# Holding back part of a weight load behind the first gather, and moving one tile's first steps forward, in a routed feed-forward kernel

## The chip, the cores and the metric

One core of a Trainium2 chip runs the whole kernel. Its engines are TensorE (PE in the profile; its weight loads are PEld), VectorE (DVE), ScalarE (ACT), GpSimd (POOL) and SyncE (SP), which here only issues transfers. The metric is the device time of one execution in microseconds, as the median of several runs. The kernel before takes 59.47 us (three runs, 58.83 to 59.89).

## The reference

```python
def _L0_cond_ref(inputs, initial_state):        # x and cond
    rates = relu(inputs) * 0.001
    c = initial_state[:, None, :] + cumsum(rates, axis=1)
    fl = floor(c)
    prev = concatenate([floor(initial_state)[:, None, :], fl[:, :-1, :]], axis=1)
    return (fl - prev) / 0.001                   # spikes

def _L0_ffn_ref(x, router_w, w1, w2):           # E = 8 experts, K = 2, HID 256, FFN 1024
    probs = softmax(x_flat @ router_w.T)
    top_v, top_i = top_k(probs, 2); top_v = top_v / sum(top_v)
    for k in range(2):
        # each token goes to expert top_i[:, k], if there is room for it
        h = gelu(expert_in @ w1[e], approximate=False)
        y = h @ w2[e]
        out = out + y[token] * (gate * keep)
    return out

return x + _L0_ffn_ref(_L0_cond_ref(x, cond), router_w, w1, w2)
```

x is 32 sequences of 64 steps and 256 channels, so 2048 tokens. A spike (0 or 1000) comes only where the running sum of a channel passes a whole number, which is rare: most tokens have no spike at all, a few have one, fewer have two. The product of such a token with w1 is one row of w1, or the sum of two rows, times 1000.

## The kernel before

**States and waves.** x lies in SBUF as 16 blocks of 128 tokens. A block's running sums are matrix products (`summed_up`, `begun`) and a floor (`floor`). Eight blocks make a *wave*; there are two. `chain(w, between)` takes one wave from its states to its indices: it finds the tokens that have a spike (`live`, `rk`), packs them (`sel`, `seld`, then the matmul of L431 and its copy to `spt`, L440), multiplies with the router's weights (L451), picks the two best experts (`best`, L473; `oh`), counts places (L485 to L494), compares them with row numbers (`strike`, L388), and multiplies that out to indices of rows of w1 (`collect`, L513; `idx`, L536 and L542).

**Tiles.** Each wave has two tiles `q`, of four experts with 32 rows each: tile 0 is wave 0 with experts 0 to 3, tile 1 wave 0 with 4 to 7, and tiles 2 and 3 the same of wave 1. For each tile GpSimd issues two gathers of rows of w1 (`bring`, L522): the first spike's rows, and the second's for those tokens that have one. `add_rows` (L891, VectorE) adds the two in place, `turn_rows` (L903, TensorE) turns the sum in pieces of 128 columns, `hidden` (L910, ScalarE) takes the GELU, and `second` (L920, TensorE) multiplies with w2 of the tile's four experts. A *quarter* is 256 of the 1024 columns, a *pair* two of the eight pieces.

**What stands between the steps.** `chain` calls `between` at named points, and what is called there is put into the engines' lists at that point. In the first wave these are the second wave's states (`second_states`); in the second wave it is `others`, with spins (`spin`, L307: products of zeros that nothing reads), VectorE's `lead` and `choices` (which of a token's two experts is first and which second), and, after the first index of the wave (`rows0`), `first_tile`: tile 0's sums, four spins, turns and GELU, and the first quarter of its second product. The indices of tile 3 (`rows1`) are multiplied out behind it. After both waves come tile 0's other three quarters, tile 1's sums, `choices(1)`, `members_told`, `weighed`, `counted` (L721), and then the other tiles.

**Who sets the order.** TensorE, VectorE, ScalarE and GpSimd run in the order of the code (`manual_schedule` names these four). SP is not named: the order of its transfers is set by a planner at build time, which keeps what depends on what and may otherwise change places. On SP stand, in this kernel, most of x, then w2 in twelve loads (experts 0 to 3 whole, 1 MB each; the first halves of experts 4 to 7, then their second halves, 0.5 MB each), then `out` = x in two stores. The last two steps add the tiles' results by indirect stores onto those rows of `out` that have spikes, and wait for these two.

```python
    parts = [(e, slice(0, FC)) for e in range(E // 2)]
    for s in (slice(0, FC // 2), slice(FC // 2, FC)):
        parts += [(e, s) for e in range(E // 2, E)]
```

The matmul's operand `w2_sb` is one tile, and each load writes its own part of it.

Of the kernel before, what the change touches and what calls it, by code (L numbers as in the profile page):

```python
# [13 lines left out]
AF = mybir.ActivationFunctionType  # L14
# [15 lines left out]
@with_exitstack  # L30
def adaln_ffn_kernel(
    ctx: ExitStack,
    tc: tile.TileContext,
    x: bass.AP,
    cond: bass.AP,
    router_w: bass.AP,
    w1: bass.AP,
    w2: bass.AP,
    out: bass.AP,
):  # L40

    nc = tc.nc
    P = 128  # L50
    B, T, H = x.shape
    E, _, FF = w1.shape
    N = B * T
    NB = N // P
    HC = H // P
    FC = FF // P
    WE = HC * FF
    assert WE == FC * H
    of = out.rearrange("b t h -> (b t) h")

    const = ctx.enter_context(tc.tile_pool(name="const", bufs=1))
    wpool = ctx.enter_context(tc.tile_pool(name="weights", bufs=1))
    dram = ctx.enter_context(tc.tile_pool(name="dram", bufs=1, space=bass.MemoryType.DRAM))


    cond_sb = const.tile([B, H], F32, name="cond_sb")
    nc.scalar.dma_start(cond_sb, cond)
    x_sb = const.tile([P, NB, H], F32, name="x_sb")
    xf = x.rearrange("b t h -> (b t) h").rearrange("(i p) h -> p i h", p=P)
    rw_sb = const.tile([E, H], F32, name="rw_sb")  # L70
    for queue, s in (
        (nc.sync, slice(0, 1)),
        (nc.scalar, slice(2, 4)),
        (nc.sync, slice(1, 2)),
        (nc.sync, slice(4, 6)),
        (nc.sync, slice(6, 8)),
        (nc.sync, slice(8, 12)),
        (nc.sync, slice(12, 16)),
    ):
        queue.dma_start(x_sb[:, s, :], xf[:, s, :])  # L80
        if s.start == 8:
            nc.sync.dma_start(rw_sb, router_w)
    w2_sb = wpool.tile([P, E * WE], F32, name="w2_sb")

    parts = [(e, slice(0, FC)) for e in range(E // 2)]
    for s in (slice(0, FC // 2), slice(FC // 2, FC)):
        parts += [(e, s) for e in range(E // 2, E)]
    for e, s in parts:
        nc.sync.dma_start(
            w2_sb[:, e * WE : (e + 1) * WE].rearrange("p (c h) -> p c h", c=FC)[:, s, :],  # L90
            w2[e].rearrange("(c p) h -> p c h", p=P)[:, s, :],
        )

    for s in (slice(0, 8), slice(8, 16)):
        nc.sync.dma_start(of.rearrange("(i p) h -> p i h", p=P)[:, s, :], x_sb[:, s, :])

    spk_dram = dram.tile([N, H], F32, name="spk_dram")
    y_dram = dram.tile([tiles_at_most(N, E, 2) * P, H], F32, name="y_dram")
    shape = (B, T, H, E, FF)
    bad_i = const.tile([P, 1], I32, name="bad_i")  # L100

    sparse(tc, x.rearrange("b t h -> (b t) h"), x_sb, cond_sb, rw_sb, w1.rearrange("e h f -> (e h) f"), w2_sb, out, bad_i, shape)
    bad = nc.values_load(
        bad_i[0:1, 0:1],
        min_val=0,
        max_val=16 * P,
        skip_runtime_bounds_check_because="it is a count of flags, at most 16 in a partition",
    )
    with tc.If(bad > 0):
        general(tc, x_sb, cond_sb, rw_sb, w1, w2_sb, out, spk_dram, y_dram, shape)  # L110


SB = 32
RE = 32


@with_exitstack
def sparse(ctx, tc, xf, x_sb, cond_sb, rw_sb, w1r, w2_sb, out, bad_i, shape):

# [8 lines left out]
    nc = tc.nc  # L130
    P = 128
# [5 lines left out]
    FC = FF // P  # L137
    WE = HC * FF
# [3 lines left out]
    W = 2  # L142
# [25 lines left out]
    warm = sc.tile([P, 4], F32, name="warm")  # L168
    nc.vector.memset(warm, 0.0)  # L169
    nc.scalar.activation(warm, warm, AF.Sqrt)  # L170
    zero = sc.tile([P, 1], F32, name="zero")
# [131 lines left out]
    def spin(n, cols=512):  # L303

        for _ in range(n):
            spun[0] += 1
            nc.tensor.matmul(wide[spun[0] % 2][:, :cols], busy.to_broadcast([P, P]), busy.to_broadcast([P, cols]), start=True, stop=True)  # L307
# [87 lines left out]
    def chain(w, between):  # L395
# [30 lines left out]
        for j in range(JW):  # L426
            t = w * JW + j
# [8 lines left out]
                        stop=True,  # L436
                    )
        for j in range(JW):
            copy = nc.vector.tensor_copy if j == 0 else nc.scalar.copy
            copy(spt[:, w * JW + j].rearrange("p c s -> p (c s)"), mid[j][:, : HC * P])  # L440
        between("spikes")

# [68 lines left out]
        def collect(out, q, s):  # L511
            for n, j in want:
                tell(  # L513
                    out,
                    slots_to_rows(n, q, j),
                    info[:, tiles(n)[j], s],
                    start=(n, j) == want[0],
                    stop=(n, j) == want[-1],
                )

        def bring(q, k):
            nc.gpsimd.indirect_dma_start(  # L522
                out=w1g[:, w, q, k, :],
                out_offset=None,
                in_=w1r,
                in_offset=bass.IndirectOffsetOnAxis(ap=idx[w][q][k], axis=0),
                bounds_check=E * H - 1,
                oob_is_err=False,
            )

        for q in range(Q):
            if q:
                for n in reversed(members[w]):
                    strike(n, q)
            collect(first[:, q : q + 1], q, slice(0, 1))
            nc.vector.tensor_scalar(  # L536
                idx[w][q][0], first[:, q : q + 1], w1_row[:, q, 0:1], E * H - 1.0, ALU.add, ALU.min
            )
            bring(q, 0)
            collect(rest[:, q], q, slice(1, 4))  # L540
            nc.vector.tensor_tensor(far[:, w, q : q + 1], rest[:, q, 0:1], w1_row[:, q, 1:2], ALU.add)
            nc.vector.scalar_tensor_tensor(  # L542
                idx[w][q][1], rest[:, q, 2:3], -FAR, far[:, w, q : q + 1], ALU.mult, ALU.add
            )
            bring(q, 1)
            between(f"rows{q}")
# [123 lines left out]
    def choices(w):  # L670
        js = slice(w * JW, (w + 1) * JW)
        nc.vector.tensor_scalar(valid[:, js], lg_w[w][:, :, E], 0.0, None, ALU.is_lt)
        nc.vector.tensor_tensor(ohk[:, 0, js], lg_w[w][:, :, :E], bc(best[:, js, 0], E), ALU.is_equal)
        nc.vector.tensor_tensor(ohk[:, 0, js], ohk[:, 0, js], ohj[w], ALU.mult)
        nc.vector.tensor_tensor(ohk[:, 1, js], ohj[w], ohk[:, 0, js], ALU.subtract)

    def others(at):
        if at == "ranks":
            spin(2)
        if at == "slots":  # L680

            nc.vector.tensor_reduce(most, cum[0].rearrange("p e j -> p j e"), AX.X, ALU.max)
            nc.vector.tensor_scalar(over, most, TOP + RE, None, ALU.is_gt)
            nc.vector.tensor_tensor(more, oh[:, 0], over.unsqueeze(1).to_broadcast([P, E, JW]), ALU.mult)
            lead(0)
            choices(0)
        if at == "spikes":
            spin(2)
        if at == "logits":
            told(1)  # L690
            spin(1)
        if at == "places":
            spin(1)
            lead(1)
            nc.scalar.activation(warm, zero[:, 0:1].to_broadcast([P, 4]), AF.Gelu)
            spin(1)
        if at == "rows0":
            first_tile()
            nc.scalar.activation(g1, gap, AF.Exp)
            nc.scalar.activation(warm, zero[:, 0:1].to_broadcast([P, 4]), AF.Gelu)  # L700
# [187 lines left out]
    def add_rows(u, s):  # L888
        w, q = order[u]
        g = w1g[:, w, q]  # L890
        nc.vector.tensor_tensor(g[:, 0, s], g[:, 0, s], g[:, 1, s], ALU.add)  # L891
# [7 lines left out]
    def turn_rows(u, cs):  # L899

        w, q = order[u]
        for c in cs:
            nc.tensor.transpose(turning(u, c, c + 1), w1g[:, w, q, 0, c * P : (c + 1) * P], ident)  # L903

    def hidden(u, cs):

        if u not in hts:
            hts[u] = big.tile([P, FC, P], F32, name=f"ht{u}")
        lo, hi = cs[0], cs[-1] + 1
        nc.scalar.activation(  # L910
            hts[u][:, lo:hi, :].rearrange("p c s -> p (c s)"), turning(u, lo, hi), AF.Gelu, scale=INV_DT
        )
# [52 lines left out]
    def quarter(n):  # L965
        return slice(n * FF // 4, (n + 1) * FF // 4)
# [4 lines left out]
    def pair(n):  # L971
        return range(2 * n, 2 * n + 2)
# [6 lines left out]

    def first_tile():  # L980

        for n in range(4):
            add_rows(0, quarter(n))
        spin(4)
        for n in range(3):
            turn_rows(0, pair(n))
            hidden(0, pair(n))
        second(0, pair(0))
        turn_rows(0, pair(3))
        hidden(0, pair(3))  # L990
# [10 lines left out]
    second(0, pair(1))  # L1001
    for n in range(2):
        add_rows(1, half(n))
    choices(1)
    members_told()
    weighed()
    second(0, pair(2))
# [442 lines left out]
```

## Time and profile before

| | |
|---|---|
| median of the runs | 59.47 us |
| the profiled execution: own time, span | 61.9 us, 59.8 us |
| busy: PE, PEld, DVE, ACT, POOL | 47.1, 28.1, 36.7, 26.8, 26.6 us |
| granted TensorE clock, mean | 0.90 |
| transfers | 15.45 MB; SP's queue 12.33, GpSimd's 2.65 |
| issue to landing, gathers of w1 | 6.7 to 7.6 us |
| issue to landing, loads of w2 | 9.0 to 12.7 us |

The profile is of one execution, whose own time is 61.9 us; the span runs from its first to its last instruction, and 2.1 us lie around it. Times in it count from the span's start. A row of a group or of the timeline names line, engine and operation, then output and inputs; what stands in brackets is how long the engine had been idle and which instruction ended that. A busy TensorE is modelled and not TensorE at its peak. The clock row gives the granted share of full speed in tenths.

### The profile page before, as it was taken

Reading aid. Unit: us, or ns where it says so; the run is one execution under the profiler, and the core shown is the slowest. Engines: PE = TensorE matmul, PEld = TensorE weight load, DVE = VectorE, ACT = ScalarE, POOL = GpSimd, SP = SyncE. Lnnn points to the kernel's source line nnn. Section 1 sums busy time; section 2 is a strip of 40 time slices with the busy share of each in tenths; the row PEclk is TensorE's granted clock in tenths of the full one; section 3 lists DMA queues with packets and bytes.
Section 4 is the critical chain, followed back from the end, with each engine's and each line's share of the span. In section 5 each row is a group of like instructions: output and inputs, shape, how many; then the busy total and the mean of one; then the engine's idle time right before and its main releaser. Section 6 shows DMA issues by size and latency. Waiting matters only on the chain.

```text
span 59.8 us, 1524 instructions
## 1 busy us (share of the span) xinstructions
PE 47.1 (79%) x513; PEld 28.1 (47%) x515; DVE 36.7 (61%) x205; ACT 26.8 (45%) x59; POOL 26.6 (44%) x69
## 2 busy tenths in 40 slices
PE   3999996999596684789997998999999999740000
PEld 1347773778353353247435574675585445210000
DVE  4787099546477771779006999999989874040000
ACT  0868486177952203751609939395009910000000
POOL 5899989495057778237406700000066000606000
PEclk9999999999999999555569999999999999997555
DMA  0699999999999999999999999999922300010200
GB/s 0 158 372 344 357 346 355 351 350 346 346 357 345 347 362 379 364 363 347 348 347 392 348 357 376 377 381 384 364 84 88 93 11 0 11 68 16 75 16 0
DMA packets 14047, 15.45 MB, mean 258 GB/s; under 512 B 1057, under 2 KB 13385, under 8 KB 14032
## 3 DMA queue, kind: packets, MB, share of 16 engines
q1 hardware_dynamic: 12368, 12.33, 63.5%
q0 software_dynamic: 1344, 2.65, 12.4%
q10 hardware_dynamic: 320, 0.30, 1.4%
q8 instruction: 6, 0.10, 0.7%
q14 instruction: 9, 0.07, 0.4%
HBM read 14.98 MB, written 2.36 MB: 290 GB/s over the span
## 4 chain that ended last, share of the span: by engine, by line
PE 69%; DVE 14%; issue 4%; ACT 2%; POOL 1%; POOLq 1%; DVEq 0%
PE wide L920 23%; PE wide L333 11%; PE wide L307 8%; PE wide L903 5%; PE mid L431 4%; PE mid L952 4%; DVE hit L388 3%; DVE ge L351 2%; DVE w1g L891 2%; PE wide L336 2%; ACT ht L910 2%; PE mid L513 2%; PE mid L333 1%; PE mid L903 1%; POOL out_dram L956 1%
## 5 line engine op out<-in xcount | busy, mean ns | idle before, releaser
L920 PE MATMUL wide<-w_sb,ht 128*32 128x256 f32 x256 | 16.3, 398 | 0.3 <-ACT ht L910 0.3
L522 POOL DMA_INDIRECT w1g<-in_L_ffn_w_dram,idx x8 | 8.8, 1098 | 9.2 <-DVE idx L542 5.1
L920 PEld LDWEIGHTS wide<-w_sb,ht 128*32 128x32 f32 x256 | 7.7, 113 | 6.2 <-issue 1.3
L333 PE MATMUL wide<-rel,trib 128*128 128x256 f32 x28 | 10.0, 472 | 0.0
L307 PE MATMUL wide<-busy 128*128 128x512 bf16 x15 | 6.6, 561 | 1.2 <-DVE warm L169 0.9
L910 ACT ACTIVATE ht<-wide 128x512 f32<-128x512 f32 (+1 forms) x8 | 4.0, 542 | 7.6 <-PE wide L903 7.6
L333 PEld LDWEIGHTS wide<-rel,trib 128*128 128x128 f32 x28 | 5.5, 228 | 2.1 <-POOL slot L229 0.9
L831 POOL DMA_INDIRECT xg<-in_x_dram,idx_x x2 | 2.0, 1012 | 9.7 <-DVE idx_s L830 9.3
L328 ACT ACTIVATE rel<-x_sb 128x512 f32<-128x512 f32 (+1 forms) x9 | 5.2, 580 | 1.8 <-DMA x_sb<-in_x_dram 1.6
L351 DVE TENSOR_SCALAR_CACHE_REDUCE ge<-wide 128x256 bf16<-128x256 f32 x11 | 4.3, 421 | 2.2 <-PE wide L336 2.0
L891 DVE TENSOR_TENSOR w1g<-w1g 128x512 f32<-128x512 f32 (+1 forms) x10 | 5.3, 579 | 0.0
L956 POOL DMA_INDIRECT out_dram<-o,idx_s x2 | 2.0, 1018 | 7.0 <-DVE o L955 7.0
L937 ACT ACTIVATE junk<-x_sb,xlim 128x1024 bf16<-128x1024 f32 x4 | 4.6, 1148 | 0.0
L903 PE MATMUL wide<-ident,w1g 128*128 128x128 f32 x28 | 4.3, 297 | 0.0
L903 PEld LDWEIGHTS wide<-ident,w1g 128*128 128x128 f32 x28 | 3.5, 153 | 1.0 <-DVE g L270 0.4
L281 POOL MEMSET w1g<- 128x1024 f32 x4 | 3.7, 949 | 0.0
L952 PE MATMUL mid<-y,back 128*128 128x256 f32 x8 | 2.8, 428 | 0.8 <-DVE y L930 0.8
L336 PE MATMUL wide<-con,selt 96*128 96x256 bf16 x14 | 3.3, 273 | 0.0
L536 DVE TENSOR_SCALAR idx<-mid,w_row 128x1 uint32<-128x1 f32 x4 | 0.9, 218 | 3.9 <-PE mid L513 3.6
L388 DVE TENSOR_TENSOR hit<-small,iota_r 128x256 bf16<-128x256 f32 x6 | 2.4, 419 | 1.1 <-PE small L494 1.1
L307 PEld LDWEIGHTS <-busy 128*128 128x128 bf16 x17 | 1.6, 120 | 2.9 <-issue 2.0
L930 DVE COPY y<-wide 128x256 f32<-128x256 f32 x4 | 1.7, 418 | 1.7 <-PE wide L920 1.7
(215 smaller groups left out, 82.2 us busy)
## 6 DMA issues: line engine op xcount, KB each, us to landing
w_sb<-in_L_ffn_w_dram SPq DMA_DIRECT2D x4, 1024.0 KB, 9.0
w_sb<-in_L_ffn_w_dram SPq DMA_DIRECT2D x8, 512.0 KB, 12.4
out_dram<-x_sb SPq DMA_DIRECT2D x2, 1024.0 KB
x_sb<-in_x_dram SPq DMA_DIRECT2D x2, 512.0 KB, 6.4
x_sb<-in_x_dram SPq DMA_DIRECT2D x2, 256.0 KB
x_sb<-in_x_dram SPq DMA_DIRECT2D x2, 128.0 KB, 2.4
x_sb<-in_x_dram ACTq DMA_DIRECT2D x1, 256.0 KB
w1g<-in_L_ffn_w_dram,idx POOLq DMA_INDIRECT x8, 6.9
```

Of the source, the lines that this page charges most:

```text
L307: nc.tensor.matmul(wide[spun[0] % 2][:, :cols], busy.to_broadcast([P, P]), busy.to_broadcast([P, cols]), start=True, stop=True)
L328: nc.scalar.activation(rel, x_sb[:, i : i + n, :], AF.Relu, scale=DT)
L333: nc.tensor.matmul(state(i), trib, rels[i], start=True, stop=False)
L336: nc.tensor.matmul(state(i), selt[:, i * nb : (i + 1) * nb, :].rearrange("p b t -> p (b t)"), con, start=False, stop=True,)
L351: nc.vector.tensor_scalar(ge[:, i, :], state(i), 1.0, None, ALU.is_ge, ALU.add, accum_out=sums[:, i : i + 1])
L522: nc.gpsimd.indirect_dma_start(out=w1g[:, w, q, k, :], out_offset=None, in_=w1r, in_offset=bass.IndirectOffsetOnAxis(ap=idx[w][q][k], axis=0),
L891: nc.vector.tensor_tensor(g[:, 0, s], g[:, 0, s], g[:, 1, s], ALU.add)
L903: nc.tensor.transpose(turning(u, c, c + 1), w1g[:, w, q, 0, c * P : (c + 1) * P], ident)
L910: nc.scalar.activation(hts[u][:, lo:hi, :].rearrange("p c s -> p (c s)"), turning(u, lo, hi), AF.Gelu, scale=INV_DT)
L920: nc.tensor.matmul(ys[u][d * RE : (d + 1) * RE, :], hts[u][:, c, d * RE : (d + 1) * RE], w2_sb[:, at : at + H], start=(c == 0), stop=(c == ...
L937: nc.scalar.activation(junk, x_sb[:, u * n : (u + 1) * n, :].rearrange("p i h -> p (i h)"), AF.Relu, bias=xlim, accum_out=xhigh[:, u : u + 1],
L952: nc.tensor.matmul(total, back[:, w, q, :], ys[u], start=(q == 0), stop=(q == Q - 1))
```

## The change

Three things are changed. On SP, the load of w2 of the first three experts (`HELD`) stays where it was; the other nine loads and `out` = x are called from inside the first wave, after its first gather, and behind a memset of one element of expert 3's part of `w2_sb` on GpSimd, which writes what that load writes. In the second wave, the sums of tile 0 are spread: two quarters after the router's product (`logits`), one at `places`, one in `first_tile`; the turns and GELUs of two of its four pairs go to `places`, and six spins leave. ScalarE's table for the GELU is loaded ahead of them. And `choices(0)` moves from the second wave to where `choices(1)` stands, while the second wave's second copy to `spt` moves from ScalarE to VectorE (of the four copies only that of wave 0's second half is left on ScalarE).

```diff
-    for e, s in parts:
-        nc.sync.dma_start(w2_sb[... e, s], w2[e][... s])
-    for s in (slice(0, 8), slice(8, 16)):
-        nc.sync.dma_start(of.rearrange("(i p) h -> p i h", p=P)[:, s, :], x_sb[:, s, :])
+    def load_w2(parts):
+        for e, s in parts:
+            nc.sync.dma_start(w2_sb[... e, s], w2[e][... s])
+    load_w2(parts[:HELD])
+    def later_loads():
+        load_w2(parts[HELD:])
+        for s in (slice(0, 8), slice(8, 16)):
+            nc.sync.dma_start(of.rearrange("(i p) h -> p i h", p=P)[:, s, :], x_sb[:, s, :])
...
+HELD = 3
...
         for j in range(JW):
-            copy = nc.vector.tensor_copy if j == 0 else nc.scalar.copy
+            copy = nc.scalar.copy if (w, j) == (0, 1) else nc.vector.tensor_copy
...
             bring(q, 0)
+            if (w, q) == (0, 0):
+                nc.gpsimd.memset(w2_sb[0:1, HELD * WE : HELD * WE + 1], 0.0)
+                later_loads()
             collect(rest[:, q], q, slice(1, 4))
...
             lead(0)
-            choices(0)
...
         if at == "logits":
             told(1)
             spin(1)
+            add_rows(0, quarter(0))
+            add_rows(0, quarter(1))
         if at == "places":
-            spin(1)
+            nc.scalar.activation(warm, zero[:, 0:1].to_broadcast([P, 4]), AF.Gelu)
             lead(1)
-            nc.scalar.activation(warm, zero[:, 0:1].to_broadcast([P, 4]), AF.Gelu)
-            spin(1)
+            add_rows(0, quarter(2))
+            for n in range(2):
+                turn_rows(0, pair(n))
+                hidden(0, pair(n))
...
     def first_tile():
-        for n in range(4):
-            add_rows(0, quarter(n))
-        spin(4)
-        for n in range(3):
-            turn_rows(0, pair(n))
-            hidden(0, pair(n))
+        add_rows(0, quarter(3))
+        turn_rows(0, pair(2))
+        hidden(0, pair(2))
         second(0, pair(0))
         turn_rows(0, pair(3))
         hidden(0, pair(3))
...
     second(0, pair(1))
     for n in range(2):
         add_rows(1, half(n))
-    choices(1)
+    for w in range(W):
+        choices(w)
     members_told()
```

## The prediction

> **What bounds the kernel now.** I read the clock and transfer rows of the page first, then the chain of waits in order of time, the timeline around the second wave, the groups of single DMA issues, and the bytes of each queue by window.
>
> ```profile
> PEclk9999999999999999555569999999999999997555
> DMA  0699999999999999999999999999922300010200
> GB/s 0 158 372 344 357 346 355 351 350 346 346 357 345 347 362 379 364 363 347 348 347 392 348 357 376 377 381 384 364 84 88 93 11 0 11 68 16 75 16 0
> ```
>
> A slice is 1.5 us. The DMA engines are full at about 350 GB/s from 2 to 43 us, so a transfer put later in the same queue lands later by its bytes. TensorE is at half clock in four slices, from 24.0 to 30.8 us.
>
> ```profile
> 23.74 0.26 DVE best L473 x2
> 26.03 1.73 PE wide L307 x4
> 29.04 1.86 PE wide L920 x16
> 31.74 0.25 PE mid L513 x4
> 32.36 1.29 DVE w1g L891 x2
> 34.82 0.17 PE small L721
> ```
>
> This is the chain of waits (start, length). The second wave picks its two best experts at 23.7; TensorE spins until the first tile's sums are there, does the first quarter of its second product at 29.0, and only behind that (TensorE takes its list in order) multiplies out the indices of the last two gathers, 31.1 to 32.0. Then VectorE adds tile 1's rows and makes the choices, and TensorE counts at 34.8. From there to 53.5 the chain is nearly all TensorE, so whatever is lost at 34.8 is lost at the end.
>
> ```profile
> 18.69 0.99 POOL L522 DMA_INDIRECT w1g<-in_L_ffn_w_dram,idx  x1 [0.31 <-DVE idx L542]
> 22.97 0.37 ACT L440 CAST spt<-mid 128x256 bf16<-128x256 f32 x1 [1.99 <-PE mid L431]
> 23.74 0.25 DVE L473 MAX8 best<-small 128x8 f32<-128x10 f32 x2 [1.61 <-PE small L451]
> 26.36 1.43 DVE L891 TENSOR_TENSOR w1g<-w1g 128x256 f32<-128x256 f32 x4
> 28.96 1.94 PE L920 MATMUL wide<-w_sb,ht 128*32 128x256 f32 x16
> ```
>
> The timeline: the sums (L891) run at 26.4 without a wait, and `best` had waited 1.6 us for ScalarE's late copy of `spt`. The second product (L920) starts at 28.96.
>
> **The order on SP.** SP is the one engine whose order is not written by hand. The built kernel's list for it reads:
>
> ```
> L91 DMACopy w_sb<-in_L_ffn_w_dram 128x8x256 x3
> L91 DMACopy w_sb<-in_L_ffn_w_dram 128x4x256 x4
> L91 DMACopy w_sb<-in_L_ffn_w_dram 128x8x256
> L91 DMACopy w_sb<-in_L_ffn_w_dram 128x4x256 x4
> ```
>
> Only the load of expert 3 overlaps the memset on GpSimd and waits. The first halves of experts 4 to 7 do not, and the planner has put all four ahead of it. So the five experts do not wait: expert 3 moves from fourth to eighth in the queue, 2.10 MB later, and four halves go earlier.
>
> What waits behind expert 3 on SP (second halves, out = x) keeps its bytes ahead of it. SP issued the load that completes the same 7.09 MB (1.84 of x, 5.24 of w2) at 17.64 in the trace. The first gather's issue runs from 17.13 to 18.38, and a memset of one element is some 0.1 us (the page's small memsets on GpSimd), so SP stands still for about 0.9 us, until 18.55. Is the queue empty then?
>
> ```profile
> q1 hardware_dynamic: 5406, 5.38, 91.7%
> q1 hardware_dynamic: 2761, 2.75, 80.0%
> L89 SPq DMA_DIRECT2D w_sb<-in_L_ffn_w_dram x2: 1381/1809/2237, 17.7 to 19.1; - x2
> DMA to landing us min/median/max: 12.0/12.0/12.0
> ```
>
> The first row is SP's queue from 0 to 18.5 us: 5.38 of 7.09 MB moved. 1.71 MB are outstanding, 4.8 us at 0.358 MB/us. The pause drains nothing, so the gathers meet the same queue as before. The second row is 18.5 to 29.2 us: together 8.13 MB, which is x (1.84) and the first eight loads of w2 (6.29). Of the two loads issued in the window of the last two rows, the eighth, issued at 19.11, lands 12.0 us later, at 31.1. Expert 3 is now that eighth load's bytes: it lands at about 31.1 where it has landed by 22.1 (20.6 to 22.1, if each load lands like its neighbours, 3 us apart per MB).
>
> **The other parts, in order of time.** (1) `choices(0)` leaves the second wave: four operations of VectorE, 21.14 to 21.79, 0.65 us off its list, and they come back behind tile 1's sums, where nothing covers them: +0.65 there. (2) Both `spt` copies go to VectorE: ScalarE's copy ended at 23.34; with the first wave's delays (0.52 and 0.70 us after L431's start) VectorE would finish both at 22.15. That alone would be worth 1.1 us at `best`. (3) But next on VectorE's list stand two quarters of tile 0's sums, in front of `best`, and they wait for both gathers of that tile. The nearest row is the second gather's:
>
> ```profile
> L522 POOL DMA_INDIRECT w1g<-in_L_ffn_w_dram,idx x1: 992/992/992, 18.7 to 18.7; - x1
> DMA to landing us min/median/max: 6.9/6.9/6.9
> ```
>
> 18.69 + 6.9 = 25.6, with the memset ahead of it 25.7. Queued behind this wait are `best`, `oh`, both strikes and the indices of the third gather; TensorE waits for `oh`. Two quarters are 0.72, so `best` is at 26.45 instead of 23.74: +2.7, and the third gather's index near 29.0 instead of 26.2 (one more quarter of 0.36 stands ahead of the strike, of which the 0.24 wait there hides most; four transposes on TensorE, 0.85 at half clock, lie beside the strikes). Third-tile rows then land near 29 + 7 = 36 to 37.5, wanted at about 38: covered, narrowly. Rule and row differ here. The Trainium skill ("DMA: Bandwidth & Descriptors", Queues, rings and completion order) has each DMA engine go round robin between its queues packet by packet; by that the gather would start at once after 18.4 and, at half of 350 GB/s, its 0.5 MB land near 21.5 to 22, and this wait would vanish. The trace says otherwise: between 18.4 and 22.0 us the gathers' queue moves nothing and SP's moves 1.23 MB. I take the trace. (4) The last quarter and turn of pair 2 leave TensorE ready for its second product at about 30.2. By the rule it would be ready near 27. In both cases it then waits for expert 3: 31.1, so the choice does not move the forecast. (5) The spins removed (six, 0.43 each at half clock) lay in front of sums that came later anyway; their gain is in (4) and is eaten by the wait.
>
> **The sum.** On the profile's own clock the second product starts at 31.1 instead of 28.96: +2.15. The turn of pair 3, the index product, tile 1's sums and the choices follow as before, +0.65 for (1): +2.8 at the count, and nothing of it comes back later, because TensorE has no slack there. Profiled execution: span 59.8 to 62.6, own time 61.9 (2.1 lie around the span) to 64.7.
>
> The median of the runs is 59.47, 2.4 below that execution. The half clock explains it: at full clock the four spins, six transposes, first quarter of the product (0.97 instead of 1.94) and the turn would have let the index product start at about 28.9 instead of 31.1, 2.2 us sooner. I take it that the timed runs do not have that stretch. With full clock in both kernels the index product is at 31.1 + 0.97 + 0.22 = 32.3 against 28.9, +3.4, and with (1) +4.05: **63.5**. With the stretch in both, 59.47 + 2.8 = 62.3. The Trainium skill ("TensorE: Matmul & The Clock Gate", Part 1: The HAM clock gate) says that an idle window of some 3.4 us halves the clock and a busy one of that length gives it back. The changed kernel would idle from about 22.8 to 27.0 and again before 31.1, so by the rule it has the half clock even where the kernel before did not: the product 1.94, the turn 0.43, 33.5 against 28.9, +4.6, and 0.65: 64.7. The trace agrees with the length (6.83 us, two windows of 3.41) but not with a simple threshold: TensorE counted as busy for 2.24 of the 3.42 us before the clock fell. So I keep 64.7 as an end, not as the forecast.
>
> **The rivals.**
> - *The hold works and the kernel is faster.* Mechanism: SP's queue runs dry before the first gather, whose rows then land as fast as the late gather of x, 3.0 us after issue with the queue nearly idle (20.1 and 21.7, the larger one 1.5 more at 350 GB/s). The sums never wait, `best` is at 22.85, the index product at about 27.3 at full clock against 28.9: −1.6, +0.65 back: 58.5. It needs nothing outstanding at 18.4. With the three loads alone (4.99 MB, moved by 17.4) that would be so; with the four halves issued it is 1.7 MB short. For it speaks only that the compiled order might not be kept by the hardware: 0.05.
> - *Expert 3 is not last.* If it lands by 30.2, because timed runs have no late DMA engine (the last of the sixteen trails by about 1.5 us), only the gather wait is left: 30.2 − 28.96 + 0.65 = +1.9, 61.4. Chance 0.06.
> - *Both waits shrink* (rows in by 24, expert 3 by 29.5), and the earlier copy pays the rest: +0.5, 60.0, no measurable change. Chance 0.06.
> - *The clock falls only in the changed kernel*: 64.7, chance 0.25. Half clock in both, 62.3: 0.2. The forecast: 0.38.
>
> **How the numbers follow.** What a measurement of this kernel can tell from no change is about 2%, 1.2 us. Slower by more: 0.38 + 0.25 + 0.2 + 0.06 = 0.89, of which 0.01 goes to no change for the small end of it; same 0.07; faster 0.05. The range goes from just under 61.4 to just over 64.7: 61.3 to 65.0.
>
> **What would show it.** Right: VectorE's first sums of tile 0 in front of `best` idle for 2.5 to 3.5 us on the gather; the first product of tile 0 waits on the load of w2, with start near 31; `choices` twice between tile 1's sums and the count; the count near 37.5. Wrong: the gathers' first packets before 20 us, expert 3's load issued before the four halves, or the index product before 31.

## The result, and the profile after

The changed kernel takes 65.91 us (median of 5 runs, 65.77 to 66.57) where the kernel before takes 59.47: 1.116 times as long, 95% interval 1.110 to 1.122. The forecast was 63.5 in a range of 61.3 to 65.0. The direction was right; the size was not, and the time lies above the range. The profiled execution takes 66.57, its span is 64.7, and its mean granted clock 0.857. Medians below are over all runs of a kernel and ratios over its undisturbed ones (three of five for the hold alone and for no hold), and some profiled executions were slower than their kernel's median: before by 2.4 us, the change by 0.7, the hold alone by 1.0, no hold by 0.9, the copy alone by 0.4. Each batch of runs had its own runs of the kernel before.

The clock and transfer rows of the page of the changed kernel; a slice is now 1.62 us:

```profile
PEclk9999999999999999555555558999999999999555
DMA  0889999999999999999999999992000330020200
GB/s 0 262 274 344 296 357 368 329 361 348 350 343 348 393 351 374 343 349 348 347 365 373 357 386 401 373 348 104 10 0 0 86 81 10 0 73 10 75 15 0
```

The transfers are as before, full until 43 us. The half clock fills eight slices and a part where it filled four: 25.76 to 39.41 us, 13.65 us instead of 6.83.

What SP did. The answers on its first held load, on the two gathers of the first tile, and SP's queue from 0 to 18.0 us (packets, MB, share of the time of 16 engines):

```profile
L91 SPq DMA_DIRECT2D w_sb<-in_L_ffn_w_dram x1: 2353/2353/2353, 17.8 to 17.8; - x1
DMA to landing us min/median/max: 13.8/13.8/13.8
```

```profile
L530 POOL DMA_INDIRECT w1g<-in_L_ffn_w_dram,idx x2: 992/1124/1257, 16.3 to 17.8; - x2
DMA to landing us min/median/max: 7.0/7.5/7.9
```

```profile
q1 hardware_dynamic: 5108, 5.08, 86.9%
```

SP had issued the four halves by 17.70 and stood still for 0.1 us until the memset. At 18.0 it had moved 5.08 of 7.09 MB: nearly all of the four halves was still queued. Expert 3 was issued at 17.81, as the eighth load, and landed 13.8 us later, at 31.65. The gathers took 7.9 and 7.0 us, where they took 6.9 before.

VectorE and TensorE around that, from the timelines:

```profile
24.91 0.76 DVE L906 TENSOR_TENSOR w1g<-w1g 128x256 f32<-128x256 f32 x2 [3.65 <-DMA w1g<-in_L_ffn_w_dram,idx]
25.59 0.24 DVE L481 MAX8 best<-small 128x8 f32<-128x10 f32 x2
```

```profile
26.11 0.18 PE L493 MATMUL small<-oh,trs 128*128 128x16 bf16 x1 [4.04 <-DVE root L503]
28.70 1.07 PE L935 MATMUL wide<-w_sb,ht 128*32 128x256 f32 x6
31.79 1.88 PE L935 MATMUL wide<-w_sb,ht 128*32 128x256 f32 x10 [2.01 <-DMA w_sb<-in_L_ffn_w_dram]
```

VectorE stands 3.65 us in front of the moved sums, and `best` comes at 25.59 instead of 23.74. TensorE stands still behind it for 4.0 us, begins the second product at 28.70 with the experts it has, and stops 2.0 us for expert 3. The chain of waits then reads:

```profile
17.81 13.84 DMA w_sb<-in_L_ffn_w_dram
31.79 1.88 PE wide L935 x10
34.76 0.25 PE mid L521 x4
35.01 4.91 PE wide L935 x48
39.92 0.11 PE small L736
```

The other three quarters of tile 0's product (48 matmuls) take 4.91 us. In the kernel before (TensorE's timeline) they took 2.80, within the time of VectorE's sums and choices:

```profile
31.91 2.80 PE L920 MATMUL wide<-w_sb,ht 128*32 128x256 f32 x48
```

The count stands at 39.92 instead of 34.82. So 5.10 us are lost by there: 2.77 up to the end of the first quarter (33.67 against 30.90), 0.25 in the turn and GELU that follow, and 2.08 from the index product to the count (5.16 against 3.08). The span grows by 4.85, so only 0.25 comes back.

Busy time in the windows of the clock, TensorE first, then (behind GpSimd) the granted clock:

```profile
22.34:25.76 3.42, 0.00 (x0) 0.00 (x0) 0.84 (x4) 0.00 (x0) 1.09 (x10) 1.00 1.05 369
25.76:29.17 3.41, 2.69 (x25) 1.60 (x24) 3.01 (x17) 2.81 (x7) 0.86 (x1) 0.50 1.11 346
29.17:32.58 3.41, 1.40 (x14) 0.41 (x9) 0.11 (x1) 0.02 (x1) 1.41 (x2) 0.50 1.10 348
32.58:36.00 3.42, 3.03 (x28) 1.59 (x27) 1.07 (x5) 1.66 (x2) 1.00 (x1) 0.50 1.07 367
36.00:39.41 3.41, 3.41 (x39) 1.58 (x32) 3.25 (x24) 1.71 (x4) 1.28 (x1) 0.50 1.09 378
```

In the first row TensorE does nothing at all, which is the wait for the gather; then the clock falls. In the third it is busy for 1.40 us, which is the wait for expert 3; full speed returns only two windows later. The first wait stands ahead of the stretch and the second falls into it. The second is not needed for its length: without the hold, where it is missing, the stretch is 13.65 us too (below).

### The profile page after: what moved, and what is told of

Its sections match the earlier page's. It is cut to its first block, busy times and chain, and to the rows that moved or that the text cites. A ratio compares the mean times of both kernels' runs of the same rounds, so it can differ in the third digit from the quotient of the medians.

```text
span 64.7 us, 1516 instructions
## 1 busy us (share of the span) xinstructions
PE 47.5 (73%) x508; PEld 27.9 (43%) x509; DVE 37.2 (58%) x206; ACT 26.2 (41%) x58; POOL 26.6 (41%) x70
## 4 chain that ended last, share of the span: by engine, by line
PE 38%; SPq 25%; DMA 21%; issue 2%; ACT 2%; DVE 1%; POOL 1%; POOLq 1%
PE wide L935 28%; DMA w_sb<-in_L_ffn_w_dram 21%; SPq L91 21%; SPq L80 4%; PE mid L967 4%; PE wide L918 4%; ACT ht L925 2%; POOL out_dram L971 1%; PE mid L918 1%; POOLq L110 1%; SPq L82 1%; DVE o L970 1%; DVE y L945 1%; PE small L799 0%; PE mid L521 0%
## 5 line engine op out<-in xcount | busy, mean ns | idle before, releaser
L935 PE MATMUL wide<-w_sb,ht 128*32 128x256 f32 x256 | 19.5, 438 | 2.3 <-DMA w_sb<-in_L_ffn_w_dram 2.0
L935 PEld LDWEIGHTS wide<-w_sb,ht 128*32 128x32 f32 x256 | 8.6, 123 | 10.4 <-issue 6.4
L341 PE MATMUL wide<-rel,trib 128*128 128x256 f32 x28 | 9.2, 437 | 0.0
L341 PEld LDWEIGHTS wide<-rel,trib 128*128 128x128 f32 x28 | 5.0, 212 | 1.8 <-POOL slot L237 0.9
L315 PE MATMUL wide<-busy 128*128 128x512 bf16 x10 | 4.1, 530 | 1.0 <-DVE warm L177 0.9
L925 ACT ACTIVATE ht<-mid 128x256 f32<-128x256 f32 x2 | 0.8, 384 | 5.3 <-PE mid L918 5.3
```

What stands on the lines that cost most here:

```text
L341: nc.tensor.matmul(state(i), trib, rels[i], start=True, stop=False)
L925: nc.scalar.activation(hts[u][:, lo:hi, :].rearrange("p c s -> p (c s)"), turning(u, lo, hi), AF.Gelu, scale=INV_DT)
L935: nc.tensor.matmul(ys[u][d * RE : (d + 1) * RE, :], hts[u][:, c, d * RE : (d + 1) * RE], w2_sb[:, at : at + H], start=(c == 0), stop=(c == ...
```

## The experiments

The spins of the experiments are products of zeros that nothing reads. `best` is its start on VectorE's timeline (the chain of waits can put it up to 0.1 later); the 48 matmuls are those behind the first quarter, by the chain where it holds them; "count" is the first matmul of `counted`; "w2 wait" is TensorE's standstill for a load of w2 in the first quarter of tile 0's product. All four are of each kernel's own profile, and those of before are of the execution of 61.9 us.

| kernel | us | before, same batch | ratio (95%) | `best` | w2 wait | 48 matmuls | count |
|---|---|---|---|---|---|---|---|
| before | 59.47 | | 1 | 23.74 | 0 | 2.80 | 34.82 |
| the change | 65.91 | 59.47 | 1.116 (1.110 to 1.122) | 25.59 | 2.0 | 4.91 | 39.92 |
| hold alone | 67.44 | 60.80 | 1.115 (1.100 to 1.129) | 23.44 | 5.7 | 4.27 | 41.7 |
| no hold | 63.33 | 60.80 | 1.047 (1.034 to 1.060) | 26.17 | 0 | 4.99 | 37.5 |
| SP in code order | 64.20 | 60.80 | none | 26.08 | 0 | 4.82 | 37.3 |
| and behind the second gather | 62.99 | 60.65 | 1.039 (1.027 to 1.050) | 23.21 | 1.4 | 3.98 | 36.0 |
| four experts early | 63.27 | 59.33 | 1.071 (1.065 to 1.076) | 25.11 | 0 | 4.35 | 35.9 |
| three and a half early | 61.53 | 59.32 | 1.038 (1.034 to 1.041) | 23.39 | 0 | 5.28 | 35.1 |

**The hold alone, and the change without it.** In the first the moved sums, turns, choices, copy and spins go back to where they were; in the second all twelve loads of w2 and the two stores are called at the start, and there is no memset.

```diff
# no hold
-    load_w2(parts[:HELD])
+    load_w2(parts)
+    # out = x, both halves, here too
...
-                nc.gpsimd.memset(w2_sb[0:1, HELD * WE : HELD * WE + 1], 0.0)
-                later_loads()
```

> The kernel before with the hold alone (three loads of w2 first, the rest behind the memset, in the order on SP that the planner then chooses), all of the first tile's steps where they were. Theory A (expert 3's load, now eighth in its queue, is the cost): the second product of tile 0 waits until about 31.7 as in the changed kernel and starts there, against 27.7 (full clock) or 29.0 (half clock) in the kernel before: 59.5 + 3 to 4 = 62.5 to 63.5, and up to 65 if the clock falls in the wait and stays at half. Theory B (the moved sums and their wait for the gathers are the cost): nothing here waits for the gathers earlier than before, so 59.5 to 60.

> The changed kernel without the hold: all loads of w2 and out = x in the order of the kernel before, no memset; the moved sums, turns, copies and choices stay. Theory A: the wait of TensorE at 28.7 to 31.8 for expert 3 is gone, the sums still wait for the gathers to about 25: 65.9 - 3.1 = 62.8, with half clock still; 61.5 if the clock comes back one window of 3.4 us sooner. Theory B: 65.5 to 66, as the changed kernel.

The hold alone costs as much as the whole change. Its `best` is even a little earlier than before, and then (TensorE's timeline):

```profile
27.93 0.63 PE L930 MATMUL wide<-w_sb,ht 128*32 128x256 f32 x6
34.22 1.88 PE L930 MATMUL wide<-w_sb,ht 128*32 128x256 f32 x10 [5.66 <-DMA w_sb<-in_L_ffn_w_dram]
```

Expert 3 was issued at 19.33 here and landed at 34.09: it was issued 1.5 us later than in the change, and the third tile's rows (0.57 MB) went in ahead of it, from 30.3 to 34.0 us. Without the hold, the moved steps cost 4.7% by themselves, by the wait for the second gather (chain of waits):

```profile
18.41 6.99 DMA w1g<-in_L_ffn_w_dram,idx
25.50 0.76 DVE w1g L904 x2
26.26 0.17 DVE best L480 x2
29.35 1.87 PE wide L933 x16
32.55 4.99 PE wide L933 x48
```

There is no wait for w2, yet the 48 matmuls take 4.99 us, because the clock is at half from 23.46 to 37.12. So each part of the change is enough to bring on the half clock, and the two losses overlap.

**The changed kernel with spins.** Fifteen more spins behind the router's product of the second wave and twelve in front of the second product, where TensorE stood still.

```diff
         if at == "logits":
             told(1)
-            spin(1)
+            spin(16)
...
         hidden(0, pair(2))
+        spin(12)
         second(0, pair(0))
```

> The changed kernel with 15 more spins (zero products of TensorE that nothing reads) after the second wave's router product and 12 ahead of tile 0's second product, so that TensorE is never idle for long between 21.6 and 31.8; its waits for the gathers and for expert 3 stay. Theory C (of the loss, some 2 us are the half clock from 25.8 to 39.4 that the two waits bring): full clock from 31.8 on, first quarter 0.97 instead of 1.88, the other three 2.8 instead of 4.9; the count then waits for VectorE, at about 37.0 instead of 39.85: 63.0. Without C: 65.5 to 66.5.

The clock stays full until 59.5 us (mean 0.975), and the 48 matmuls take 2.80 (TensorE's timeline):

```profile
33.95 2.80 PE L935 MATMUL wide<-w_sb,ht 128*32 128x256 f32 x48
37.44 0.17 PE L736 MATMUL small<-cc,trs 128*128 128x8 bf16 x1 [0.69 <-DVE what L759]
```

The time is 64.88 us, without an interval. The change by its ratio would be 1.116 × 60.8 = 67.8 in this batch, so by this estimate about 2.9 us are the half clock's, less what the spins cost: the last of them ended at 27.0, about 0.6 after `oh`. In the profiles the count is at 37.44 instead of 39.92, 2.5 earlier, and the span is 2.0 shorter. The two waits are still paid, and the other 0.5 goes behind the count, where a new end has moved in (chain of waits):

```profile
30.69 7.61 DMA w1g<-in_L_ffn_w_dram,idx
38.40 1.29 DVE w1g L906 x2
```

The third tile's rows land at 38.3, and VectorE waits 0.4 us for them.

**SP in the order of the code.** One line puts SP among the engines whose order is written by hand; a second version also calls the memset and the held list behind the second gather of tile 0 instead of the first.

```diff
# both, among the engines of manual_schedule
+                mybir.EngineType.SP,
# second version only
             bring(q, 0)
-            if (w, q) == (0, 0):
-                nc.gpsimd.memset(...)
-                later_loads()
...     (behind the second gather)
+            if (w, q) == (0, 0):
+                nc.gpsimd.memset(...)
+                later_loads()
```

> The changed kernel with SP's order also taken from the code: expert 3's load stands directly behind the memset and everything else of the held list behind it. Only 4.99 MB are then issued ahead of the first gather. Theory A with the rival of the prediction (the hold works once the order is kept): SP's queue is dry by 17.4, the first two gathers land near 20 and 21.5, best is near 22.6, expert 3 lands near 25, the index product of the last tile is at about 27.5: 58.0 to 59.0, with the two-choices cost of 0.65 in it. If the moved sums cost by themselves, or the dry stretch of about 2 us is paid at the end: 61 or more.

> As full_hold (SP in the order of the code), but the memset and the held list come behind the first tile's second gather instead of its first. Theory D (what the sums wait for is the second gather, and it is late because SP's loads are let go 0.2 us before it is issued): both gathers now meet empty DMA engines and land by 21 and 22, the sums end by 22.6, best is at 22.7 against 25.6 to 26.1, expert 3's load starts 1.3 us later than in full_hold and lands near 25, the last tile's index product is near 28. Against the kernel before: 1 us less to 1 us more, ratio 0.98 to 1.02, the more the longer the clock is at half. If D is false, 1.05 as no_hold.

In the first version SP's queue runs empty while the first gather is being issued: its first packet moves at 18.58 and its rows are in at 20.9. But SP's loads were let go at 18.01, the second gather was issued at 18.19, and it took as long as ever:

```profile
18.19 7.12 DMA w1g<-in_L_ffn_w_dram,idx
25.40 0.76 DVE w1g L907 x2
26.16 0.17 DVE best L482 x2
```

With the hold one gather later, the packets of both gathers are in by 22.1, the sums start at 22.54 without a wait, and `best` is at 23.21. What is left is the wait for expert 3 and the half clock, from 24.29 to 34.53:

```profile
26.31 1.07 PE L936 MATMUL wide<-w_sb,ht 128*32 128x256 f32 x6
28.77 1.89 PE L936 MATMUL wide<-w_sb,ht 128*32 128x256 f32 x10 [1.39 <-DMA w_sb<-in_L_ffn_w_dram]
31.93 4.05 PE L936 MATMUL wide<-w_sb,ht 128*32 128x256 f32 x48
```

Spins in this version (two at `places`, four ahead of the turn of pair 2) gave 62.28 us against 60.65, without an interval; the half clock shrank from 10.24 to 6.83 us.

> As hold_two, with two spins ahead of the turns at the second wave's places and four ahead of the turn of pair 2, as the kernel before has them. If the half clock is what is left to pay in hold_two, this is up to 2 us faster than it, 0.96 to 0.99 of the kernel before; if hold_two already has full clock, 0.5 to 1 us slower than it, for the spins stand in TensorE's list.

**The copy alone, and `choices(0)` put back.** The kernel before with only the second wave's second `spt` copy on VectorE; and the changed kernel with `choices(0)` back in the second wave.

```diff
# the copy alone
-            copy = nc.vector.tensor_copy if j == 0 else nc.scalar.copy
+            copy = nc.scalar.copy if (w, j) == (0, 1) else nc.vector.tensor_copy
# choices put back
             lead(0)
+            choices(0)
...
-    for w in range(W):
-        choices(w)
+    choices(1)
```

> The kernel before with one edit of the change alone: the second wave's second copy to spt on VectorE instead of ScalarE. ScalarE's copy began 1.4 us after its matmul was done in the trace of before; VectorE's would end near 22.1 to 22.6 instead of 23.34, so best and all behind it come 0.7 to 1.2 us sooner: 0.98 to 0.99 of the kernel before. If ScalarE's delay is only in the profiled execution, or if the sums are then what is late (tile 0's gathers land at 25.6), 1.00.

> The changed kernel with the second wave's choices for wave 0 back where they were. The prediction charged their move with 0.65 us on the path: then the count comes 0.65 sooner relative to the index product of the last tile (31.7 to 39.85 in the changed kernel). If TensorE at half clock is the later of the two at the count, as the trace of the changed kernel suggests (48 products until 39.9, the count's input ready on VectorE by 38.1): no difference, the distance stays at about 5.8 us from the index product to the count.

The copy is worth nothing: 61.04 us, ratio 1.0009 (0.997 to 1.005). VectorE's copy waits just as ScalarE's did, about 2.1 us after the start of L431 (timelines of TensorE and VectorE):

```profile
20.50 0.66 PE L431 MATMUL mid<-seld,ge 128*128 128x32 bf16 x16 [0.16 <-ACT seld L422]
22.64 0.42 DVE L440 CAST spt<-mid 128x256 bf16<-128x256 f32 x1 [0.85 <-PE mid L431]
```

So the delay does not hang on the engine that copies. `choices(0)` put back does not bring its 0.65 us either, as far as one run can tell: 67.47 us, a span of 65.7, and from the index product to the count 4.9 us (35.82 to 40.71), against 5.16; the 48 matmuls, 4.64 against 4.91, are the difference. In the changed kernel VectorE is done with the choices at 37.8, under the 48 matmuls that last until 39.9.

**Four experts early, and three and a half.** Both with SP in code order and the hold behind the second gather. Expert 3 whole, then only its first half (all that the first quarter of the product reads), goes ahead of the hold.

```diff
# four
-HELD = 3
+HELD = 4
# three and a half
-    parts = [(e, slice(0, FC)) for e in range(E // 2)]
+    parts = [(e, slice(0, FC)) for e in range(HELD)]
+    parts += [(HELD, slice(0, FC // 2)), (HELD, slice(FC // 2, FC))]
...
-    load_w2(parts[:HELD])
+    load_w2(parts[: HELD + 1])
```

> As hold_two, but four loads of w2 stay ahead (expert 3's too) and only experts 4 to 7 and out = x are held behind the second gather. If hold_two's rest is expert 3's load (1.4 us of wait at 28.8, and the third half-clock window that the wait brings): the wait is gone, the gathers start about 1 MB (3 us) of queue later than in hold_two but still land by 23, best near 23.5, the product near 26.5 without a wait: 0.98 to 1.01 of the kernel before, depending on the clock. If expert 3's load is not what hold_two pays: 1.03 to 1.04 again.

> As four_two, with four more spins behind the second wave's router product and three ahead of the turn of pair 2, where TensorE waits for VectorE anyway. If the half clock is the rest: granted clock 0.92 to 0.95 as in the kernel before, 0.97 to 0.99 of its time, faster than four_two by 0.5 to 2 us. If the clock is full in four_two already: equal to it, or 0.3 us slower.

> The held list with the memset behind the second gather, SP in the order of the code, and expert 3's load of w2 cut into two halves, of which the first stands ahead of the hold (3.5 experts early, 0.5 MB more than with three). Theory: a gather's first packet waits until SP's queue is empty, about 1.5 us later than with three experts (18.3 there, 20.4 with four), so near 19.5; the second gather's rows are in by 23.3 to 23.8, best near 24.2, and the first quarter of tile 0's product (which needs only the first half of expert 3) begins near 27.3 without the wait of 1.4 us that it had with three; index product near 29.5, count near 35.0 to 35.5 with half clock: 1.02 to 1.035 of the kernel before. Rival: half an expert costs as much at the gather as a whole one; then as with four experts early, product at 28.3, 1.06 to 1.07.

Four were expected to be enough and were not (1.071): the wait moved from w2 to the rows. The first gather packet moves at 20.35, as SP's queue runs out, against 18.25 with three early:

```profile
17.65 6.69 DMA w1g<-in_L_ffn_w_dram,idx
24.44 0.76 DVE w1g L907 x2
```

With spins (four behind the router's product, three ahead of the turn of pair 2) it gave 62.99 us, 1.063 (1.056 to 1.070): the 48 matmuls are back at 2.80, but the last three spins themselves took 1.44 us on the chain at half clock. Three and a half are the best of the three: rows at 22.62, for which VectorE stands 1.55 us, and no wait for w2. Behind that the chain of waits is TensorE at half clock, from 24.84 to 35.08:

```profile
17.74 4.88 DMA w1g<-in_L_ffn_w_dram,idx
22.71 0.76 DVE w1g L909 x2
26.57 1.87 PE wide L938 x16
29.77 5.28 PE wide L938 x48
```

**And that with the clock kept.** Four more spins between the packing and the router's product; then also six behind the router's product and two behind the first turns.

```diff
         if at == "spikes":
-            spin(2)
+            spin(6)
# the last version also
         if at == "logits":
             told(1)
-            spin(1)
+            spin(7)
...     (behind the two turns at "places")
+            spin(2)
```

> The same with four more spins between the second wave's packing product and the router's product, where TensorE stood still and nothing waits for it. Theory: if the clock's fall at 24 us is what is left of the loss, the 48 products take 2.8 to 3.0 us instead of about 4, the count is near 34.0 to 34.5, and the time is 1.00 to 1.02 of the kernel before. Rival: the clock falls a window later all the same (TensorE waits for rows and GELU again between 25 and 27), and the time is that without the spins, or above it by up to 0.5 us where the spins delay the router's product.

> The version with 3.5 experts early and four more spins, with six more spins behind the router's product of the second wave (TensorE stands still there for 1.5 us until oh) and two more behind the first two turns (idle 0.6 us until the strike). Theory: what is left of the loss, 2.8%, is the half clock between 26.0 and 32.8 us, so with the clock kept the first quarter of tile 0's product takes 1.0 instead of 1.9 us and the 48 products 2.8 instead of 3.9; the count comes near 32 instead of 34.3, and the time is 0.98 to 1.00 of the kernel before, unless the third tile's gather (rows near 36, as in the changed kernel with spins) then bounds it: 0.995 to 1.015. Rival: the clock falls all the same, and nothing changes (1.02 to 1.035); or the clock is kept and the count stays near 34, because VectorE's sums and choices set it: then the moved sums themselves are what costs, 1.02 to 1.03.

Four spins: 61.02 us, 1.028 (1.021 to 1.035), count at 34.3, half clock from 25.99 to 32.81 only. With an interval, no version came nearer. All twelve: 62.49 us, 1.053 (1.042 to 1.065), although the clock is full until 58.9 and the count is at 32.96. That is 1.9 us earlier than in the profile of before, but not early: a run of this batch's 59.2 us, with the same 2.1 around the span and 25.0 from the count to its end, would count at about 32.1 (an estimate). And behind the count 27.9 us go by. VectorE's timeline says why:

```profile
36.81 1.29 DVE L910 TENSOR_TENSOR w1g<-w1g 128x512 f32<-128x512 f32 x2 [3.26 <-DMA w1g<-in_L_ffn_w_dram,idx]
```

The third tile's rows are wanted at 33.5 and land at 36.7; VectorE's list runs late from there to the end. A part of that is the spins' own: the last two waited 1.38 us for a GELU to free the PSUM buffer that they write, and the third gather's index came at 26.76 instead of 25.60. With 1.16 us off, the wait would still be about 2.1 by this estimate, so the bound would stand. No version beats the kernel before.

## Why the prediction was wrong in size

*The order on SP, and expert 3 as eighth load.* Right. It landed at 31.65 (31.1 forecast), issued at 17.81 and not at 19.1 or later, but 13.8 us under way and not 12.0: the two errors nearly cancel. The pause was 0.1 us where 0.9 was forecast; it drained nothing in either case. The hold alone costs 1.115, but there expert 3 lands 2.4 us later than in the change.

*The moved sums wait for the second gather.* Right in kind: 3.65 us idle, `best` at 25.59 where 26.45 was forecast (the first wave ran 0.85 sooner). Here row and rule were set against each other, and the row held: gathers issued at 16.3 and 17.8 moved their first packet at 21.2, and landed at 24.2 and 24.8.

*Both copies on VectorE, worth 1.1 us at best.* The reason was wrong. The delay was taken for ScalarE's; the copy alone gives 1.0009. In the changed kernel both copies are done by 21.3, but `best` waits for the gather anyway.

*`choices(0)` costs 0.65 where nothing covers it.* Wrong: the 48 matmuls at half clock covered it. With the clock kept, TensorE does wait for VectorE at the count, 0.69 us in each of the two versions whose clock stayed full (0.11 in the profile of before).

*The third tile's rows "covered, narrowly".* Right for the changed kernel. They became the end in the versions with spins that kept the clock.

*The clock.* **This is the step that failed.** The prediction took the timed runs of both kernels at full clock, gave the half clock in the changed kernel alone a chance of 0.25 at 64.7, and kept as an end the rule of the Trainium skill ("TensorE: Matmul & The Clock Gate", Part 1: The HAM clock gate) that an idle window of some 3.4 us halves the clock. In the changed kernel the row agrees with it: a window of 3.42 us with TensorE busy for 0.00, then half clock. For the kernel before, the assumption fits roughly: of its 51 runs in the later batches 35 have a mean clock of 0.93 to 0.97, and without the stretch in the middle the profiled one would have 0.90 + 6.83 × 0.5 / 59.8 = 0.957 (0.93 with one window of 3.41 us at half clock). That the stretch cost 2.2 us there is not borne out: in the batch with 23 runs, those at 0.897 and 0.898 took 61.2 to 61.7 us, those at 0.981 to 0.983 took 60.5 to 60.6, and three at 0.974 to 0.976 took 61.2 to 61.5. For the changed kernel the assumption fails: all five runs have 0.856 to 0.879. With its own forecast of an idle stretch "from about 22.8 to 27.0 and again before 31.1", which is close to what happened (22.1 to 26.1, 29.8 to 31.8), the half clock was the case to forecast and not an end.

And the case at 64.7 was itself too small, by the length of the stretch. It priced the half clock on the first quarter's product and one turn, as if it ended there. It lasted until 39.41, and so raised the cost of the 48 matmuls, which the sum had left under VectorE's work: 4.91 instead of 2.80, and the bound of the last stretch before the count. In the trace's terms: forecast +2.8 at the count on the profile's clock, measured +5.1. The late expert gave 2.77 and the turn 0.25 where 2.15 was forecast; the matmuls gave 2.08 where 0.65 was forecast for the choices. For the medians: forecast +4.05, measured +6.44. Against the case at 64.7, the tile's first index product came at 34.08 where 33.5 was forecast (+0.58, from the later landing), and the matmuls add 2.08 − 0.65 = 1.43: 66.7, beside 66.57 for the profiled execution.

What stays open: how much the moved sums would bring with the clock kept and the third tile's rows in time. No run had both. Nor was the later hold, behind the second gather, run without the moved sums.

## What to carry to other kernels

Where a change puts a new wait of some microseconds in front of TensorE, ask first whether the clock falls in it, and price everything that TensorE does until it is back, above all what was hidden beside another engine's work. A wait put on one transfer holds back only what is queued behind it in the order as built: read that order, and then ask which bytes are still outstanding when the transfer that is to profit is issued. And when a gather and a load compete, a half of the load may be all that the next step needs.

## What the runs showed of the hardware

- Half clock came in whole windows: 3.41 and 6.83 us (hold alone), 10.24 (three and a half early), 13.65 (the change, no hold), 17.07 (choices put back). It came after windows with TensorE busy for 0.00 of 3.42 us (the change) and, in the hold alone, for 2.27 of 3.41; yet there the clock stayed full after a later window with 1.63. After a window with 3.03 busy it stayed at half in the change and came back with the hold behind the second gather. So the busy time that the profile counts does not decide it alone.
- The gathers' first packet moved at 18.25 with three experts ahead of them, 18.44 with three and a half, 20.35 with four and 21.2 in the change, for gathers issued from 16.1 to 16.3 in each. With SP's queue full (before, the change, no hold, the copy alone) it moved 3.6 us after the gather's issue had ended, and SP moved 1.24 or 1.25 MB in between. In the change 0.9 MB of what SP had issued ahead was then still outstanding, so the gather did not wait for an empty queue. A load that SP was let to issue 0.2 us before the second gather was enough to hold that gather back to 7.1 us; let go behind it, its packets were in 4.2 us after its issue.
- The copy of the second half of the second wave's `spt` is released some 2 us after its matmul's start in most kernels here (2.14 with the copy alone, 2.20 with three early), whichever engine copies; in the change and with three and a half or four early both copies were through 1.3 us after it. What decides it was not found.
